# Query, key and value projections as seven products of quarters, with the first norm's residual affine on GpSimd and the adjacency check on ScalarE

## The chip, the cores and the metric

The kernel runs on one core of one Trainium2 chip. The metric is the device time of one launch in microseconds (us). A core has a matrix engine (TensorE, PE in the profile, with its weight loads listed apart as PEld), a vector engine (VectorE, DVE), an activation engine (ScalarE, ACT), a general engine (GpSimd, POOL) and a queue engine that issues most transfers (SyncE, SP). Each engine works through its own instructions in order and waits on semaphores for the others. All data are 32-bit floats, apart from the adjacency, which is int32.

## What is computed

64 graphs of 256 nodes with 256 features go through a graph-attention layer (two attentions, two norms, a feed-forward block) and then through a relational attention layer, again with two norms and a feed-forward block. What the change touches is the start of the second layer and the norm of the first:

```python
# layer 0, after its two graph attentions
h = _layernorm(residual + h, g_ln1, b_ln1)
residual2 = h
ff = jnp.matmul(jax.nn.relu(jnp.matmul(h, w_ff1) + b_ff1), w_ff2) + b_ff2
src = _layernorm(residual2 + ff, g_ln2, b_ln2)
# layer 1
q = (src @ Wq + bq).reshape(Bb, Nn, h, dh).transpose(0, 2, 1, 3)
k = (src @ Wk + bk).reshape(Bb, Nn, h, dh).transpose(0, 2, 1, 3)
scores = jnp.einsum('bhid,bhjd->bhij', q, k) / np.sqrt(dh)
attn = jax.nn.softmax(scores, axis=-1)
for r in range(Wv.shape[0]):
    v_r = (src @ Wv[r] + bv[r]).reshape(Bb, Nn, h, dh).transpose(0, 2, 1, 3)
    mask = (adj_matrix == r)[:, None]
    out = out + jnp.einsum('bhij,bhjd->bhid', attn * mask, v_r)
```

There are 8 heads of 32 features. The adjacency holds only 0 and 1, so of the four relations two matter.

## The kernel before

`narrow_path` does the work. It assumes that the adjacency holds 0 and 1 and that no exponential overflows; it sums up evidence against that, and `general_path` runs as well if there is any.

**Tiling.** Two graphs (512 nodes) are one unit; there are 32 units. A tile has 128 partitions. Features-first tiles (`hT`) have two blocks of 128 features, each with 512 nodes; nodes-first tiles (`y`, `v`) have four blocks of 128 nodes.

**The loop.** `turn(y_, x_, z)` is called 32 times. It takes unit y_ through layer 1, unit x_ = y_+1 through the feed-forward block of layer 0, and unit z = y_+2 through the graph attentions, and weaves the three together. Within a turn the order on PE, SP, DVE and ACT is the program's own, written out by hand (`manual_schedule`); GpSimd is ordered by the framework. The last turn has no x_, and there only PE and SP have the written order.

**The start of a turn** is what the change rewrites. `query(0)`, `query(1)`, `key(0)`, `key(1)` (`projection`, L986) each multiply two 128x128 weight blocks with 512 nodes into one PSUM bank, and ACT copies the bank out while it adds the bias (L988). `scores(0)` (L1015) makes the scores of the first four heads of the first graph, and ACT takes their exponentials (L1021). `values` (L999) multiplies four blocks of nodes with 512 weight columns, and DVE adds the bias row on the way out (L1001). The norm of unit x_ is applied by ACT (`applied_norm`, L828), DVE transposes it (L668), and twelve transfers and four GpSimd copies put the blocks in place (L685). The residual's affine, y*g+b, is on DVE: `times` (L837) here and `plus` (L840) later in the turn. `masks(n)` (L1026) multiplies exponentials with the adjacency, `totals(n)` (L1031) adds the two halves of nodes, and `sums(n)` (L1041, L1044) multiplies both with the values and with ones. `first(...)` are steps of the feed-forward block's hidden layer.

**Seven products.** `hidden_seven` (L871, L880, L883) and `HiddenOut` (L960, L968) already multiply two by two quarters with seven instead of eight products. Their sums of weight quarters are formed once (`seven`, `seven_out`), those of the data in every turn by DVE (L854, L946).

**PSUM.** Of eight banks six rotate under the tag "g"; "po" and "zo" are one bank each and take the attention's sums.

**The check** (`checked`, L706) is one DVE instruction per unit near the end of a turn: the sum of (a-1)*a over the adjacency, which is 0 for zeros and ones.

**Weights.** The second norm's scale and shift of layer 0 are folded into the weights of layer 1 at the start (`folding`): `scaled` on GpSimd, `shifted` by small products.

Of the kernel before, what the change touches and what calls it, by code (L numbers as in the profile page):

```python
# [16 lines left out]
P = 128  # L17
# [368 lines left out]
def narrow_path(  # L386
# [123 lines left out]
    def gat_weights():  # L510
# [5 lines left out]
        a1, a2 = columns([v.rearrange("f o -> (f o)") for v in (g_a1, g_a2)], "ga", nc.scalar, "k")  # L516
# [31 lines left out]
    lg1, lb1, bf1, lg2, lb2, bq, bk, lg3, lb3, b1 = columns(  # L548
        (g_g1, g_b1, g_bf1, g_g2, g_b2, t_bq, t_bk, t_g1, t_be1, t_b1), "cols", nc.scalar, "q")
    rg1, rb1, rg2, rb2 = row(g_g1, "rg1"), row(g_b1, "rb1"), row(g_g2, "rg2"), row(g_b2, "rb2")  # L550

    wq, wk, wo = weight(t_Wq, "wq"), weight(t_Wk, "wk"), weight(t_Wo, "wo")
# [4 lines left out]
    rbv = row(t_bv[0:2].rearrange("r f -> (r f)"), "rbv")  # L557
    nc.vector.tensor_tensor(wv[:, :, 1, :], wv[:, :, 1, :], wv[:, :, 0, :], ALU.subtract)
    nc.vector.tensor_tensor(rbv[:, F:], rbv[:, F:], rbv[:, :F], ALU.subtract)
# [3 lines left out]
    def seven(w, name):  # L563


        h = FF // 2
# [34 lines left out]
    wf1s, wf2s, w1s, w2s = [], [], [], []  # L601

    def folding():
# [8 lines left out]
        for w, bias, name in ((wq, bq, "bq"), (wk, bk, "bk")):  # L612
            shifted(w, range(KB), lb2, bias, name)
            scaled(w, lg2)
        yield
        ps = bank("rbvp")
        for k in range(KB):
            nc.tensor.matmul(ps, lb2[:, k:k + 1].to_broadcast([P, P]), wv[:, k].rearrange("p r f -> p (r f)"),
                             start=(k == 0), stop=(k == KB - 1))
        nc.vector.tensor_tensor(rbv, rbv, ps, ALU.add)  # L620
        scaled(wv.rearrange("p c r f -> p c (r f)"), lg2)
# [12 lines left out]
    for n, (rb, v) in enumerate(((rb1, g_bf2), (rb2, t_bo), (rb3, t_b2))):  # L634
        nc.gpsimd.tensor_add(rb, rb, row(v, None, rows[:, n, :F]))

# [25 lines left out]

    def normed_features(u, l, xn, natural=False, queues=(nc.sync,)):
# [7 lines left out]
        if natural:  # L671
            hT = work.tile([P, KB, TN], F32, tag="hT", name=f"hT{u}_{l}")
            to = hT.rearrange("c k (t a r) -> c (k t) a r", a=Q, r=32)
            for q in range(Q):
                for a in range(Q):
                    move = nc.gpsimd.tensor_copy if q == a else nc.sync.dma_start
                    move(to[q * 32:(q + 1) * 32, :, a], yt[a * 32:(a + 1) * 32, q].rearrange("c k t r -> c (k t) r"))  # L677
            return [hT[:, k] for k in range(KB)]
# [25 lines left out]
    def checked(u, aq):  # L704
        a = aq.rearrange("p t n -> p (t n)")
        nc.vector.scalar_tensor_tensor(a, a, 1.0, a, op0=ALU.subtract, op1=ALU.mult,  # L706
                                       accum_out=other[:, u:u + 1])
# [20 lines left out]
    class Softmax:  # L728

        def __init__(s, u, l, wh, rows, c):  # L730
            s.u, s.wh, s.rows, s.c = u, wh, rows, c
            s.s = (work.tile([P, T, N], F32, tag="s", name=f"s{u}_{l}", bufs=1) if u > 1 else
# [98 lines left out]
    def affine(y, g_, b_):  # L831

        times(y, g_)
        plus(y, b_)

    def times(y, g_):
        nc.vector.tensor_mul(y, y, g_[:, None, :].to_broadcast(list(y.shape)))  # L837

    def plus(y, b_):
        nc.vector.tensor_add(y, y, b_[:, None, :].to_broadcast(list(y.shape)))  # L840
# [138 lines left out]
    def projection(u, hT, name, w, c):  # L979

        d = work.tile([P, KB, TN], F32, tag=name, name=f"{name}{u}", bufs=1)

        def step(m):
            ps = bank(f"{name}p{u}_{m}")
            for k in range(KB):
                nc.tensor.matmul(ps, w[:, k, m * P:(m + 1) * P], hT[k],  # L986
                                 start=(k == 0), stop=(k == KB - 1))
            nc.scalar.activation(d[:, m, :], ps, AF.Identity, bias=c[:, m:m + 1])  # L988

        return d, step  # L990

    def values(u, hT, blocks, v=None):
        if v is None:
            v = work.tile([P, T, 2 * F], F32, tag="v", name=f"v{u}", bufs=1)
        wvf = wv.rearrange("p c r f -> p c (r f)")
        for t in blocks:
            ps = bank(f"vp{u}_{t}")
            for k in range(KB):
                nc.tensor.matmul(ps, hT[k][:, t * P:(t + 1) * P], wvf[:, k, :],  # L999
                                 start=(k == 0), stop=(k == KB - 1))  # L1000
            nc.vector.tensor_tensor(v[:, t, :], ps, rbv, ALU.add)  # L1001
        return v
# [3 lines left out]
    def weighted(u, b, m, q, k_, aT):  # L1006
# [13 lines left out]
        for a in range(HPB):  # L1020
            mark[f"exp{b * KB + m}"] = nc.scalar.activation(e[:, a, :], ps[a], AF.Exp, scale=isd)  # L1021
        return b, m, ab, e, ea
# [24 lines left out]
    def divided(u, b, po, zo, oT):  # L1047


        rz = work.tile([P, KB * N], F32, tag="s" if u < NG - 1 else "yt", name=f"rz{u}_{b}", bufs=1)  # L1050
# [62 lines left out]
    def out_pieces(u, y, h1):  # L1113

        if u == NG - 2:
            s = [work.tile([P, T, N], F32, tag="s", name=f"sq{u}", bufs=1),
# [38 lines left out]
    def turn(y_, x_, z):  # L1155
# [3 lines left out]
        q, query = projection(y_, hT, "q", wq, bq)  # L1159
        k_, key = projection(y_, hT, "k", wk, bk)  # L1160
        oT = q
        acc = [None] * G
        e = {}

        def scores(n):
            e[n] = weighted(y_, *quads[n], q, k_, Y["aT"])
# [31 lines left out]
        with order:  # L1198
            query(0)
            query(1)  # L1200
            if X:
                applied_norm(X["y"], *X.pop("n"))
            last = norm(waiting[0][0], 3, waiting[0][1]) if waiting else None
            key(0)
            key(1)
            if X:
                X["hT"] = normed_features(x_, 0, X["y"])
                times(X["y"], rg1)
            scores(0)
            if z + 1 < NG:  # L1210
                load_x(z + 1)
            if X:
                masks(0)
                totals(0)
# [278 lines left out]
```

## Time and profile before

| | |
|---|---|
| Time of the launch | 3075.3 us, median of 3 runs (3073.74 to 3075.54) |
| Profiled execution | span 3072.8 us |
| One turn, from one first query product to the next (1510.36 to 1604.16) | 93.80 us |
| PEld busy | 2330.1 us (76%) |
| DVE busy | 2595.7 us (84%) |
| ACT busy | 1602.2 us (52%) |
| POOL busy | 648.0 us (21%) |
| Granted TensorE clock, mean | 0.995 |
| L837 y*g on DVE, 128x1024 | 126 times, mean 1263 ns |
| L840 y+b on DVE, 128x1024 | 126 times, mean 1302 ns |
| L706 check on DVE, 128x1024 | 30 times, mean 1216 ns |
| L685 GpSimd copy, 32x256 | 386 to 1442 ns, median 400 |

An engine's busy time is the union of its instructions' durations. Matrix instructions overlap in the pipe, so what one costs is read from the distance of starts and not from its duration. A 32-bit product appears as two records: 512 records of L999 are 32 turns times four blocks of nodes times two blocks of features times two.

### The profile page before, as it was taken

How to read it: one execution, taken by the hardware profiler on the slowest of the kernel's cores; microseconds unless marked ns; L12 is line 12 of the kernel's file. 1: busy time of each engine (PE TensorE's matmuls, PEld its weight loads, DVE VectorE, ACT ScalarE, POOL GpSimd, SP SyncE). 2: the span in 40 equal slices, each digit the busy share in tenths (PEclk: the TensorE clock that was granted, in tenths of full speed). 3: DMA queues.
4: the chain of work that ended last, by engine and by line, in shares of the span. 5: the costliest groups of instructions: out<-in, count | busy, mean ns of one | idle time of the engine just before them, and what ended most of it. 6: DMA issues, size and time to landing. Idle time of an engine off the chain costs nothing.

```text
span 3072.8 us, 56424 instructions
## 1 busy us (share of the span) xinstructions
PE 3031.3 (99%) x21432; PEld 2330.1 (76%) x21432; DVE 2595.7 (84%) x4890; ACT 1602.2 (52%) x3212; POOL 648.0 (21%) x896
## 2 busy tenths in 40 slices
PE   7999999999999999999999999999999999999998
PEld 6677877778777778777787777787777787777866
DVE  4788888888888888888888888888888888888876
ACT  4455545555545555555555455555455554554553
POOL 3122121222211221212221112222112212122211
PEclk8999999999999999999999999999999999999999
DMA  5011111211111211112211112111112111121000
GB/s 149 13 37 35 34 39 25 44 41 35 35 35 32 44 37 32 39 26 43 44 33 35 40 25 44 37 36 35 30 38 44 35 34 39 25 44 37 18 13 16
DMA packets 427988, 113.37 MB, mean 37 GB/s; under 512 B 364568, under 2 KB 427072, under 8 KB 427712
## 3 DMA queue, kind: packets, MB, share of 16 engines
q1 hardware_dynamic: 417664, 102.46, 15.8%
q10 hardware_dynamic: 8992, 6.19, 0.8%
q8 instruction: 172, 2.82, 0.4%
q0 software_dynamic: 1056, 1.05, 0.1%
q14 instruction: 104, 0.85, 0.1%
HBM read 57.04 MB, written 16.78 MB: 24 GB/s over the span
## 4 chain that ended last, share of the span: by engine, by line
PE 90%; DVE 7%; DMA 1%; POOL 1%; ACT 1%; issue 0%; SPq 0%; ACTq 0%; POOLq 0%; DVEq 0%
PE yf L960 22%; PE h1a L871 15%; PE h1b L871 11%; PE po L1041 8%; PE vp L999 7%; PE sp L1015 4%; PE xpp L715 4%; PE yop L786 4%; PE qp L986 3%; PE kp L986 3%; PE ygp L786 3%; PE zo L1044 2%; PE hpp L775 2%; DVE s L750 2%; DVE yt L668 1%; DVE eaq L946 1%
## 5 line engine op out<-in xcount | busy, mean ns | idle before, releaser
L880 ACT COPY h<-h1b 128x512 f32<-128x512 f32 x384 | 224.6, 585 | 390.0 <-PE h1b L871 390.0
L828 ACT ACTIVATE y<-y,nm,rs 128x256 f32<-128x256 f32 x450 | 239.0, 591 | 238.4 <-DVE nm L821 234.1
L883 DVE TENSOR_TENSOR h<-h1a,h 128x512 f32<-128x512 f32 x384 | 263.6, 687 | 117.5 <-PE h1a L871 111.6
L1026 DVE TENSOR_TENSOR ea<-e,aT 128x1024 f32<-128x1024 f32 x256 | 309.5, 1239 | 54.3 <-ACT e L1021 54.3
L1021 ACT ACTIVATE e<-sp 128x512 f32<-128x512 f32 x512 | 264.3, 602 | 52.0 <-PE sp L1015 48.7
L1054 POOL TENSOR_TENSOR low<-low,rq 128x16 f32<-128x16 f32 x64 | 13.9, 218 | 1087.3 <-DVE rq L1053 1087.3
L685 POOL COPY hT<-yt 32x256 f32<-32x256 f32 x244 | 207.2, 849 | 59.0 <-DVE yt L668 51.4
L968 DVE TENSOR_TENSOR y<-yf,y 128x256 f32<-128x256 f32 x448 | 183.1, 409 | 39.7 <-PE yf L960 39.6
L999 PE MATMUL vp<-wv,hT 128*128 128x512 f32 x480 | 214.0, 599 | 0.0
L801 DVE BATCH_NORM_STATS2 st<-y 128x6 f32<-128x256 f32 x512 | 207.7, 408 | 5.5
L812 POOL TENSOR_SCALAR rs<-mv 128x4 f32<-128x4 f32 (+1 forms) x134 | 34.2, 255 | 720.7 <-DVE mv L802 454.6
L999 PEld LDWEIGHTS vp<-wv,hT 128*128 128x128 f32 x480 | 88.7, 190 | 110.4 <-issue 103.2
L840 DVE TENSOR_TENSOR y<-y,rb 128x1024 f32<-128x1024 f32 (+1 forms) x130 | 166.9, 1284 | 3.2
L988 ACT ACTIVATE q<-qp,cols 128x512 f32<-128x512 f32 x64 | 44.0, 687 | 238.3 <-PE qp L986 238.3
L914 ACT ACTIVATE h<-h,cols 128x512 f32<-128x512 f32 x256 | 167.0, 714 | 1.5 <-DVE h L883 1.1
L837 DVE TENSOR_TENSOR y<-y,rg 128x1024 f32<-128x1024 f32 (+1 forms) x130 | 161.8, 1245 | 2.2 <-ACT y L828 1.1
L1031 DVE TENSOR_TENSOR es<-e 128x1024 f32<-128x1024 f32 x128 | 155.5, 1215 | 0.0
L677 POOL COPY hT<-yt 32x256 f32<-32x256 f32 x120 | 115.6, 964 | 169.2 <-DVE yt L668 159.7
L1015 PEld LDWEIGHTS sp<-q,k 32*128 32x128 f32 x2048 | 92.5, 184 | 74.2 <-issue 44.8
L1015 PE MATMUL sp<-q,k 32*128 32x256 f32 x2048 | 146.6, 400 | 2.0 <-ACT k L988 2.0
L1041 PE MATMUL po<-e,v 128*32 128x256 f32 x2048 | 136.3, 384 | 0.0
L813 POOL TENSOR_TENSOR rs<-rs,mhalf 128x4 f32<-128x4 f32 (+1 forms) x134 | 134.5, 1004 | 8.2
(249 smaller groups left out, 7191.4 us busy)
## 6 DMA issues: line engine op xcount, KB each, us to landing
hT<-yt SPq DMA_DIRECT2D x912, 32.0 KB, 2.0
y<-in_x_dram SPq DMA_DIRECT2D x32, 512.0 KB, 4.7
xq<-in_x_dram SPq DMA_DIRECT2D x240, 64.0 KB, 2.2
aq<-in_adj_dram SPq DMA_DIRECT2D x240, 64.0 KB, 2.4
out_dram<-y SPq DMA_DIRECT2D x30, 512.0 KB, 2.9
hT<-yt ACTq DMA_DIRECT2D x180, 32.0 KB, 1.9
wf<-in_L_gnn_w_ff_dram SPq DMA_DIRECT2D x2, 1024.0 KB, 8.1
w<-in_L_gnn_W_dram SPq DMA_DIRECT2D x2, 1024.0 KB
```

Of the source, the lines that this page charges most:

```text
L786: nc.tensor.matmul(ps[:, i * F:(i + 1) * F], lhs(t, k), rhs(b, k), start=(k == 0), stop=(k == n - 1))
L801: nc.vector.bn_stats(st[:, t, :], y[:, t, :])
L828: mark["normed"] = nc.scalar.activation(y[:, t, :], y[:, t, :], AF.Identity, bias=nm[:, t:t + 1], scale=rs[:, t:t + 1])
L871: nc.tensor.matmul(ps[:, i * N:(i + 1) * N], w_[:, f * P:(f + 1) * P], m, start=first and i == 0, stop=True, skip_group_check=True)
L880: mark["copied"] = nc.scalar.copy(out(h, o, b), pair(ps))
L883: mark["added"] = nc.vector.tensor_tensor(out(h, o, b), pair(one[h]), out(h, o, b), ALU.add)
L960: nc.tensor.matmul(s.ps[n][:, i * F2:(i + 1) * F2], a[:, k, i * P:(i + 1) * P], w_[:, k, :], start=n in (1, 2, 5) and i == 0 and k == 0, s ...
L999: nc.tensor.matmul(ps, hT[k][:, t * P:(t + 1) * P], wvf[:, k, :], start=(k == 0), stop=(k == KB - 1))
L1015: nc.tensor.matmul(ps[a][:, j * N:(j + 1) * N], k_[hp, m, j0:j0 + P], q[hp, m, b * N:(b + 1) * N], start=True, stop=True)
L1021: mark[f"exp{b * KB + m}"] = nc.scalar.activation(e[:, a, :], ps[a], AF.Exp, scale=isd)
L1026: nc.vector.tensor_tensor(ea[:, a:a + 2, :], e[:, a:a + 2, :], ab[:, None, :].to_broadcast([P, 2, NB * N]), ALU.mult)
L1041: nc.tensor.matmul(po[hp, m * N:(m + 1) * N], vs[:, hp], w[:, a, j * N:(j + 1) * N], start=(n == 0), stop=(n == len(terms) - 1))
```

## The change

Query, key and value are made by a class `Projections`. The weights of query and key are joined to one 256x512 matrix, those of the two relations' values to another, and each is multiplied with the unit's features as two by two quarters, in seven products. One product is two 128x128 blocks times 256 columns. Results go through two PSUM banks: for query and key two of "g", for the values "zo" and "po". ACT copies four times per matrix, DVE adds three times. Four sums of data quarters are made by DVE at the start of a turn. The biases are no longer added on the way out: one feature row of the data (partition 96 of the second block) is set to 1 by GpSimd (`with_ones`), and the weights' row there holds the bias. Since normalized features sum to zero, that feature's weights are subtracted from all rows first (`joined`). The steps of the start are woven anew. Both parts of the residual's affine after the first norm go to GpSimd. The check is an ACT instruction, Square of a-0.5 with an accumulator, which is 0.25 for each zero or one; it stands earlier, behind the second softmax's exponentials. Two buffers are shared anew (tags "s" and "k" go).

```diff
+    def joined(w, name, bias):
+        ps, pr = bank(f"{name}bp"), bank(f"{name}rp")
+        for k in range(KB):
+            nc.tensor.matmul(ps, lb2[:, k:k + 1].to_broadcast([P, P]), w[:, k],
+                             start=(k == 0), stop=(k == KB - 1))
...
+        nc.tensor.matmul(pr, only.to_broadcast([P, P]), w[:, KB - 1], start=True, stop=True)
+        nc.vector.tensor_tensor(bias, bias, ps[one].rearrange("p (o f) -> p o f", o=2), ALU.add)
+        for k in range(KB):
+            nc.vector.scalar_tensor_tensor(w[:, k], w[:, k], lg2[:, k:k + 1], pr,
+                                           op0=ALU.mult, op1=ALU.subtract)
...
-        for w, bias, name in ((wq, bq, "bq"), (wk, bk, "bk")):
-            shifted(w, range(KB), lb2, bias, name)
-            scaled(w, lg2)
+        joined(wqk, "wqk", brow[:, 0:2])
+        wqks.extend(seven(wqk, "wqk"))
         yield
...
+        joined(wvf, "wv", brow[:, 2:4])
+        wvs.extend(seven(wvf, "wv"))
...
+    def with_ones(hT):
+        nc.gpsimd.memset(hT[KB - 1][one], 1.0)
+        return hT
...
     def checked(u, aq):
         a = aq.rearrange("p t n -> p (t n)")
-        nc.vector.scalar_tensor_tensor(a, a, 1.0, a, op0=ALU.subtract, op1=ALU.mult,
-                                       accum_out=other[:, u:u + 1])
+        nc.scalar.activation(a, a, AF.Square, bias=mhalf[:, 0:1], accum_out=other[:, u:u + 1])
...
-            s.s = (work.tile([P, T, N], F32, tag="s", name=f"s{u}_{l}", bufs=1) if u > 1 else
+            s.s = (work.tile([P, T, N], F32, tag="v", name=f"s{u}_{l}", bufs=1) if u > 1 else
...
+    def affine(y, g_, b_, engine=None):
+        engine = engine or nc.vector
+        engine.tensor_mul(y, y, g_[:, None, :].to_broadcast(list(y.shape)))
+        engine.tensor_add(y, y, b_[:, None, :].to_broadcast(list(y.shape)))
...
+        def sums(s):
+            tt = work.tile([P, HPB, NB * N], F32, tag="e", name=f"tq{s.u}").rearrange("p a n -> p (a n)")
+            s.t = [tt[:, n * N:(n + 1) * N] for n in range(4)]
+            for n, (x_, y_) in enumerate(((s.h[0][1], s.h[0][0]), (s.h[1][1], s.t[0]),
+                                          (s.h[1][1], s.h[0][1]), (s.h[1][0], s.t[1]))):
+                nc.vector.tensor_tensor(s.t[n], x_, y_, ALU.subtract)
...
+        def copied(s, x, o, b, ps):
+            nc.scalar.copy(s.out(x, o, b), ps.rearrange("p (i n) -> p i n", i=2))
+        def added(s, x, o, b):
+            y = s.out(x, o, b)
+            nc.vector.tensor_tensor(y, s.one[x].rearrange("p (i n) -> p i n", i=2), y, ALU.add)
+        def step(s, x, n):
+            a11, a12, a22, s1, s2, s3, s4 = wqks if x == "q" else wvs
+            w, m = {1: (a11, s.h[0][0]), 2: (a12, s.h[1][0]), 5: (s1, s.t[0]), 3: (s4, s.h[1][1]),
+                    6: (s2, s.t[1]), 7: (s3, s.t[2]), 4: (a22, s.t[3])}[n]
...
+            ps = (s.two if n in (2, 5, 3) else s.one)[x]
+            for i in range(2):
+                l, r = (w[:, i * P:(i + 1) * P], m) if x == "q" else (m[:, i * P:(i + 1) * P], w)
+                nc.tensor.matmul(ps[:, i * N:(i + 1) * N], l, r, start=n in (1, 2, 5) and i == 0, stop=True,
+                                 skip_group_check=True)
+            if n == 2:
+                s.copied(x, 0, 0, ps)
+                s.added(x, 0, 0)
+            elif n == 5:
+                s.copied(x, 1, 1, ps)
+            elif n == 3:
+                s.copied(x, 0, 1, ps)
+            elif n == 6:
+                s.added(x, 0, 1)
+            elif n == 7:
+                s.added(x, 1, 1)
+            elif n == 4:
+                s.copied(x, 1, 0, ps)
...
         with order:
-            query(0)
-            query(1)
+            p.sums()
+            p("q1 v1 q2")
             if X:
-                applied_norm(X["y"], *X.pop("n"))
+                applied_norm(X["y"], *X["n"], [0, 1])
             last = norm(waiting[0][0], 3, waiting[0][1]) if waiting else None
-            key(0)
-            key(1)
+            p("v2 q5")
             if X:
+                applied_norm(X["y"], *X.pop("n"), [2, 3])
                 X["hT"] = normed_features(x_, 0, X["y"])
-                times(X["y"], rg1)
-            scores(0)
+                affine(X["y"], rg1, rb1, nc.gpsimd)
+            scores(0, ())
+            p("v5")
+            powers(0, (0, 1))
             if z + 1 < NG:
                 load_x(z + 1)
-            if X:
-                masks(0)
-                totals(0)
-            v = values(y_, hT, range(0, T // 2))
...
+            p("q3 v3")
+            masks(0, (0,))
+            powers(0, (2, 3))
             if waiting:
                 applied_norm(waiting[0][1], *last)
-            if X:
-                v = values(y_, hT, range(T // 2, T), v)
+            p("q6 v6 q7 v7")
+            masks(0, (2,))
+            totals(0)
+            p("q4 v4")
             steps = first_hidden(x_) if X else None
             scores(1)
...
+            masks(1)
+            totals(1)
             if Z:
                 early(z)
-            masks(1)
-            totals(1)
             sums(0)
...
-            if X:
-                plus(X["y"], rb1)
             scores(3)
...
             Z["m"].exp(0)
             Z["m"].exp(1)
+            checked(z, Z["aq"])
+            if z + 1 < NG:
+                load_adjacency(z + 1)
             out.add(5)
...
             affine(X["y"], rg2, rb2)
             out(7)
-            checked(z, Z["aq"])
-            if z + 1 < NG:
-                load_adjacency(z + 1)
```

## The prediction

> **What bounds the kernel now.** I read the page's busy times first, then the chain that ended last, then the turn that begins at 1510.36 us in the chain and in the engines' timelines.
>
> ```profile
> PE 3031.3 (99%) x21432; PEld 2330.1 (76%) x21432; DVE 2595.7 (84%) x4890; ACT 1602.2 (52%) x3212; POOL 648.0 (21%) x896
> ...
> PE 90%; DVE 7%; DMA 1%; POOL 1%; ACT 1%; issue 0%; SPq 0%; ACTq 0%; POOLq 0%; DVEq 0%
> ```
>
> The matrix engine is the bound; DVE is next, with 79 us of work in a turn of 93.8. A busy PE says little about its efficiency, so the price of a product is read from the chain, whose pieces are distances between starts (start, us, what, records):
>
> ```profile
> 1510.36 3.44 PE qp L986 x8
> 1513.80 3.43 PE kp L986 x8
> 1517.23 1.08 PE sp L1015 x16
> 1518.31 7.07 PE vp L999 x16
> 1525.37 1.07 PE sp L1015 x16
> 1526.45 1.86 PE po L1041 x32
> ...
> 1536.05 0.86 PE h1a L871 x4
> ```
>
> A record of 512 columns takes 0.43 us (3.44/8), one of 256 takes 0.215 (0.86/4). The values take 7.07 and not 16 x 0.43 = 6.88: the first product behind the scores' narrow ones pays about 0.17. The start of the turn up to the attention's first sums is 16.09 us with no gap.
>
> Where DVE has room there is shown by its waits (start, us, and in brackets the idle time before):
>
> ```profile
> 1606.84 0.16 DVE L821 SCALAR_TENSOR_TENSOR nm<-mv,rs 128x4 f32<-128x4 f32 x1 [1.24 <-POOL rs L813]
> ...
> 1613.24 2.58 DVE L1026 TENSOR_TENSOR ea<-e,aT 128x1024 f32<-128x1024 f32 x2 [1.20 <-ACT e L1021]
> ...
> 1628.85 0.72 DVE L1052 STREAM_TRANSPOSE rz<-zo 128x512 f32<-128x512 f32 x1 [2.36 <-PE zo L1044]
> ```
>
> Up to the second sums of a turn DVE is 2.4 us ahead of PE, and after that it works without a pause. So a saving on PE must keep within what DVE and ACT can follow in those first 24.6 us.
>
> **What the skill says.** "TensorE: Matmul & The Clock Gate", Back-to-back issue gap, has a warm product cost its columns at 2.4 GHz plus 2.5 ns. Halving the width therefore loses next to nothing, and the 0.43 and 0.215 above agree. "SBUF — State Buffer", Who interferes with whom, says that a DVE instruction with two SBUF inputs and a GpSimd instruction that reads SBUF exclude each other, for the whole instruction. The trace agrees, at its start:
>
> ```profile
> 43.69 1.74 POOL L570 TENSOR_TENSOR wf1s<-wf1s,wf 128x512 f32<-128x512 f32 x1
> 45.39 1.71 POOL L572 TENSOR_TENSOR wf<-wf 128x512 f32<-128x512 f32 x1
> ...
> 45.90 1.49 DVE L750 SCALAR_TENSOR_TENSOR s<-s,aT 128x256 f32<-128x256 f32 x1
> 47.32 0.08 DVE L750 DVE_READ_ACCUMULATOR s<-s,aT 128x1 f32 x1
> 47.32 1.48 DVE L750 SCALAR_TENSOR_TENSOR s<-s,aT 128x256 f32<-128x256 f32 x1
> 48.73 0.08 DVE L750 DVE_READ_ACCUMULATOR s<-s,aT 128x1 f32 x1
> 48.73 0.41 DVE L750 SCALAR_TENSOR_TENSOR s<-s,aT 128x256 f32<-128x256 f32 x1
> ```
>
> The same DVE instruction takes 0.41 us alone and 1.49 beside a two-input GpSimd one of 512 elements: that one holds the port about 1.0 us, and it gets it between two DVE instructions. "ScalarE: Activation LUTs", Table sets, says that cheap functions lie in every set; it does not name Square there.
>
> **The projections on PE.** Removed: 3.44 + 3.43 + 7.07 = 13.94 us. Added: 2 x 7 products of 4 records, 56 x 0.215 = 12.07, and 0.17 behind the scores. Gross gain 1.70 us a turn, 54 us in 32 turns, if nothing waits.
>
> **What PE waits for instead.** I lay out the new start by the written order, counted from its first product (0.86 us a product, 0.2 from a release to the product that needed it, as a freed PSUM bank also has its weights to load).
> Products q1, v1, q2, v2, q5 end at 4.31; the scores end at 5.39. ACT copies q2 from 2.63 to 3.22 (0.59, as L880), DVE adds until 3.95 (0.69, as L883), then makes nm (0.16), and only then may ACT apply two blocks of the norm (0.59 + 0.49) ahead of v2's copy, which ends at 5.75. v5 writes the bank that this copy frees: it starts at 5.93 where 5.56 was possible. Loss 0.37.
> v3 needs v5's copy, which stands behind the norm's other two blocks and ends at 7.80: loss 0.35.
> q7 needs DVE's add for q6; ahead of it in DVE's order stand the first mask (1.2), which waits for two exponentials (to 8.85), and nm. The add ends at 10.9, q7 starts at 11.05 instead of 10.6: loss 0.45, or 0.77 if GpSimd copies take the port ahead of the mask and of nm. I take 0.45.
> The rest of the row has its adds in time. The second scores end at 15.6, the first sums start there instead of at 16.09: of the 1.70 some 0.5 is left (0.2 with the high value).
>
> **DVE and ACT beside it.** DVE gains work in this stretch: four sums (1.7, from four times L854's 0.42) and six adds of 0.69 for four of 0.68 (+1.4), less `times` (1.26). That uses up the lead of 2.4 but not more. `plus` (1.30) and the check (1.22 + 0.08) also leave DVE, in places where PE does not wait for it, so I count no gain. With the check gone from the turn's end DVE reaches the four sums about 1 us earlier, in time for q5. ACT gets eight copies for four (8 x 0.59 - 4 x 0.68 = 2.0 us) and the check, about 1 us by the spacing of its 512-element rows. The check falls into this hole:
>
> ```profile
> 1597.56 1.71 ACT L766 ACTIVATE hp<-hp,z 128x256 f32<-128x256 f32 x4 [3.86 <-DVE z L754]
> ```
>
> If Square needed another table, 1.28 us more fits there, and the load back for the next exponentials falls before the next turn's first copy. SP gets the adjacency's eight transfers earlier; behind them on SP there is nothing until the next norm's twelve, a turn's start later. The ones row on GpSimd comes some 12 us before its use. So both: nothing.
>
> **The affine on GpSimd.** No row shows a two-input GpSimd instruction of 1024 elements beside DVE work. From 1.27 us at 512 elements with 1.0 of it on the port I estimate 2.3 us with 2.0 on the port, each. They follow the four copies: transposes end near 8.25, copies near 10.8 (0.4 each, one shut out by the mask), multiply until 13.2, add until 15.5. The multiply meets DVE at adds that read PSUM, which have one SBUF input and pass. The add meets the second half of the masks, due at 13.5, and holds it until about 15.3. Then masks end at 16.5 and totals at 17.7; PE wants them at 16.5 and 17.4. So 0.15 to 0.35 is lost; none with 1.6 on the port, 0.85 with 2.3. I take 0.2. The hidden layer's four sums and the next masks then run without a gap and end about when the second sums need them.
>
> **Start and sum.** `joined` adds six wide products (12 records, 5.2 us) and drops 16 one-column records (0.115 each) and four wide ones (3.7 together); GpSimd forms eight sums of 0.85 where it scaled for 3.8. I count +1 us once. Per turn 0.5 - 0.2 = 0.3, for 31 turns 9.3; the last turn has no affine and may keep 1.0. Sum: 9.3 + 1.0 - 1 = 9.3 us off the profiled span of 3072.8. The launch's median lies 2.5 above that span, which I keep: 3075.3 - 9.3 = 3066.
>
> **The rivals.**
> Slower: the affine's add holds the port for 2.3 us or starts later, the q7 wait is at its high end, and each hand-over costs a little more. The mechanism is one: DVE gets to `masks` and `totals` too late for the first sums. It decides once DVE is delayed more than the 1.7 us of lead that it has there. With 0.2 left of the gain and 0.6 lost, +0.4 x 31 = 12 us: 3088. For it speaks the port in the trace; against it, that PE's own waits before the sums give DVE time.
> No difference: waits give back all of the 1.70, 3075. For it speaks that every hand-over above is within 0.3 us of being in time or late.
> Large gain: the waits at v5 and v3 do not arise as laid out (ACT a little earlier) and the port is free; 1.3 of 1.70 stays, 40 us: 3035. Against it, ACT's written order.
> The change does not do what it says: if the new check counted wrongly, the general path would run as well, far above all of this.
>
> **Chances.** A measurement of this kernel tells about 0.2%, 6 us, from no change. Forecast (a gain of 6 to 25 us) 0.40; large gain 0.10; no difference 0.17; slower by DVE's delay 0.32; general path 0.01. Faster 0.50, same 0.17, slower 0.33. The range 3040 to 3093 leaves out the upper end of the large gain and delays above 0.6 us a turn; the forecast's own range is 3050 to 3069.
>
> **What would show it.** PE's first row: 56 records in about 13.4 us with gaps before v5, v3 and q7. DVE: a mask or total of 1.2 us drawn out to 2.5 to 3.5 beside a GpSimd add. The first sums 15.4 to 16.0 us after the turn's start, the second ending at 24.2 to 24.6 (24.62 now). A turn of 93.5 us. I am wrong if PE waits in the feed-forward steps have changed too, if tables are loaded more than 64 times, or if GpSimd's instructions take over 3 us.

## The result: slower by 0.3%, where a gain was forecast

| | before | after |
|---|---|---|
| Time of the launch, median of 7 runs each on one chip | 3074.53 us (3073.05 to 3076.28) | 3083.82 us (3082.2 to 3085.53) |
| Profiled span | 3072.8 us | 3083.0 us |
| A turn, median of turns 1 to 29 | 93.44 us | 93.63 us |
| First sums start, from the turn's first product | 16.18 us | 15.80 us |
| `zo` of the first pair ends | 18.54 us | 18.74 us |

The ratio is 1.003, with a 95% interval of 1.002 to 1.004. The forecast was 3066; the slower case had 3088. Positions in a turn are here read from the engines' timelines, where the old first sums start at 16.18 us and not at 16.09, as the chain has it.

The profiled spans differ by 10.2 us. Start of the first turn: 0.44 us earlier. First turn: 1.25 longer. The 29 turns behind it: 0.19 each by their medians, 5.5, and 0.9 more in single longer turns. Last turn but one: 0.2 longer. Last turn: 2.7 longer. The parts come to 10.1, and rounding explains the rest.

DVE's group of totals on the page of the kernel before:

```profile
L1031 DVE TENSOR_TENSOR es<-e 128x1024 f32<-128x1024 f32 x128 | 155.5, 1215 | 0.0
```

On the page of the kernel after, the busy times, the share of each engine in the chain, and the same group:

```profile
PE 3011.8 (98%) x22192; PEld 2459.0 (80%) x22192; DVE 2626.4 (85%) x4963; ACT 1684.3 (55%) x3404; POOL 845.3 (27%) x992
...
PE 80%; DVE 13%; SPq 2%; issue 2%; ACT 2%; DMA 1%; POOL 1%; DVEq 0%; POOLq 0%; ACTq 0%
...
L1095 DVE TENSOR_TENSOR es<-e 128x1024 f32<-128x1024 f32 x128 | 220.9, 1726 | 0.0
```

PE's busy time fell by 19.5 us although the launch became longer, and DVE's share of the chain rose from 7% to 13%. The totals are about half of that rise (3% of the chain on that page). One took 1215 ns on average before and takes 1726 now; 128 of them make 65 us, which is 2.1 us for one total in each of 31 turns. In the trace it is the first total of a turn: in turns 1 to 29 it takes 3.38 to 3.40 us, and the second takes 1.22.

The chain of waits of the kernel after, for a turn (start, us, what):

```profile
1609.25 0.87 PE qk L1046 x4
1610.12 0.86 PE v L1046 x4
...
1623.14 0.58 SPq L713
1623.72 0.04 issue
1623.76 0.06 SPq L713
1623.83 3.32 DVE es L1095
1627.15 0.04 issue
1627.19 0.64 PE zo L1108 x8
```

A product of four records costs the expected 0.86 to 0.88 us where nothing waits. What ends last is no product but the first pair's total: 3.32 us on DVE, for which PE's `zo` waits. SP's transfers stand ahead of it in the chain but don't release it: the total reads exponentials alone.

The timeline of the same turn shows what draws the total out (start, us, engine, line, what; in brackets the idle time before). The first product starts at 1609.09:

```profile
1614.91 1.13 PE L1046 MATMUL v<-wvs,tq 128*128 128x256 f32 x4 [0.18 <-ACT v L1029]
...
1617.43 2.75 POOL L711 COPY hT<-yt 32x256 f32<-32x256 f32 x4 [0.49 <-DVE yt L694]
...
1619.97 1.13 PE L1046 MATMUL qk<-tq,wqk 128*128 128x256 f32 x4 [0.26 <-DVE qk L1033]
1620.26 2.36 POOL L859 TENSOR_TENSOR y<-y,rg 128x1024 f32<-128x1024 f32 x1
1622.61 1.21 DVE L1090 TENSOR_TENSOR ea<-e,aT 128x1024 f32<-128x1024 f32 x1
1622.69 3.36 POOL L860 TENSOR_TENSOR y<-y,rb 128x1024 f32<-128x1024 f32 x1
1623.74 3.39 DVE L1095 TENSOR_TENSOR es<-e 128x1024 f32<-128x1024 f32 x1
1627.19 0.64 PE L1108 MATMUL zo<-es,ones 128*32 128x256 f32 x8 [0.37 <-DVE es L1095]
```

GpSimd's multiply (L859) takes 2.36 us, and the add (L860) is issued 0.08 us behind the second half of the mask. The mask passes in its usual 1.21 us; the add waits for it and takes 3.36. The total, queued behind the mask, then waits for the add: 3.39 us for an instruction of 1.22. So the port (the access to SBUF that the two engines share, as the prediction has it) goes back and forth, and each side waits once for nearly the whole of the other's instruction.

### The profile page after: what moved, and what is told of

Same layout as the page of the kernel before. It is cut to its first block, busy times and chain, and to the rows that moved or that the text cites. A ratio compares the mean times of both kernels' runs of the same rounds, so it can differ in the third digit from the quotient of the medians.

```text
span 3083.0 us, 58504 instructions
## 1 busy us (share of the span) xinstructions
PE 3011.8 (98%) x22192; PEld 2459.0 (80%) x22192; DVE 2626.4 (85%) x4963; ACT 1684.3 (55%) x3404; POOL 845.3 (27%) x992
## 4 chain that ended last, share of the span: by engine, by line
PE 80%; DVE 13%; SPq 2%; issue 2%; ACT 2%; DMA 1%; POOL 1%; DVEq 0%; POOLq 0%; ACTq 0%
PE yf L980 22%; PE h1a L891 15%; PE h1b L891 11%; PE po L1105 6%; PE qk L1046 4%; PE xpp L740 4%; PE yop L811 4%; PE ygp L811 3%; PE v L1046 3%; DVE es L1095 3%; PE sp L1077 2%; PE zo L1108 2%; PE hpp L800 2%; SPq L713 2%; DVE yt L694 2%
## 5 line engine op out<-in xcount | busy, mean ns | idle before, releaser
L1029 ACT COPY qk<-qk 128x512 f32<-128x512 f32 x128 | 75.4, 589 | 287.6 <-PE qk L1046 287.6
L1095 DVE TENSOR_TENSOR es<-e 128x1024 f32<-128x1024 f32 x128 | 220.9, 1726 | 0.0
L1077 PE MATMUL sp<-qk 32*128 32x256 f32 x2048 | 146.6, 400 | 0.1
L742 ACT COPY xp<-xpp 128x260 f32<-128x260 f32 x128 | 45.5, 386 | 171.6 <-PE xpp L740 171.5
L1033 DVE TENSOR_TENSOR qk<-qk,qk 128x512 f32<-128x512 f32 x96 | 65.9, 687 | 84.1 <-ACT qk L1029 64.9
L891 PE MATMUL h1a<-tt,wf 128*128 128x256 f32 x512 | 134.2, 386 | 0.0
L1105 PE MATMUL po<-ea,v 128*32 128x256 f32 x2048 | 134.2, 379 | 0.0
L980 PEld LDWEIGHTS yf<-wf,eaq 128*128 128x128 f32 x1024 | 119.1, 192 | 16.1 <-DVE eaq L966 14.9
```

The lines of the kernel that those rows point to most:

```text
L891: nc.tensor.matmul(ps[:, i * N:(i + 1) * N], w_[:, f * P:(f + 1) * P], m, start=first and i == 0, stop=True, skip_group_check=True)
L980: nc.tensor.matmul(s.ps[n][:, i * F2:(i + 1) * F2], a[:, k, i * P:(i + 1) * P], w_[:, k, :], start=n in (1, 2, 5) and i == 0 and k == 0, s ...
L1077: nc.tensor.matmul(ps[a][:, j * N:(j + 1) * N], k_[hp, m, j0:j0 + P], q[hp, m, b * N:(b + 1) * N], start=True, stop=True)
L1095: mark[f"summed{b * KB + m}"] = nc.vector.tensor_add(es, e[:, :, 0:N], e[:, :, N:2 * N])
L1105: nc.tensor.matmul(po[hp, m * N:(m + 1) * N], vs[:, hp], w[:, a, j * N:(j + 1) * N], start=(n == 0), stop=(n == len(terms) - 1))
```

## The experiments

Every kernel has 4 to 21 runs; the kernel before ran beside it on the same chip (19 to 28 runs), and the ratio is to those. "Turn" is the median of turns 1 to 29 of the profiled execution, "excess" what those turns have above 29 times that median (2.4 in the kernel after, 1.5 in the kernel before), "sums" and "zo" the start of the first sums and the end of the first pair's `zo`. In the expectations P is the theory that GpSimd holds the port when DVE needs it, F that the features land too late for the hidden layer, W that the written order makes PE wait.

| Run | Median, us | Ratio (95%) | Turn | Excess | Sums | zo |
|---|---|---|---|---|---|---|
| no_affine | 3070.91 | 0.9988 (0.9981 to 0.9995) | 93.07 | 9.6 | 15.79 | 18.16 |
| affine_late | 3082.82 | 1.0026 (1.0016 to 1.0037) | 93.63 | 2.3 | 15.80 | 18.74 |
| affine_dve | 3090.89 | 1.0053 (1.0039 to 1.0066) | 93.91 | 2.2 | 16.65 | 19.01 |
| before_affine_pool | 3172.72 | 1.0321 (1.0307 to 1.0335) | 96.11 | 17.5 | 18.84 | 21.21 |
| affine_low | 3072.51 | 0.9992 (0.9984 to 1.0) | 93.06 | 7.2 | 15.79 | 18.16 |
| add_low | 3070.27 | 0.9985 (0.9979 to 0.9992) | 93.05 | 6.5 | 15.79 | 18.16 |
| affine_low_feat | 3088.31 | 1.0045 (1.0031 to 1.0059) | 93.80 | 0.6 | 15.79 | 18.16 |
| affine_low_q7 | 3081.05 | 1.0018 (1.001 to 1.0027) | 93.53 | 1.3 | 15.53 | 17.89 |
| affine_low_last | 3087.32 | 1.004 (1.0027 to 1.0054) | 93.80 | 0.1 | 15.80 | 18.16 |
| affine_low_third | 3067.29 | 0.9973 (0.9962 to 0.9984) | 93.06 | 1.3 | 15.80 | 18.16 |
| affine_low_best | 3044.87 | 0.9901 (0.9886 to 0.9916) | 92.40 | 1.7 | 15.14 | 17.50 |
| before_check_act | 3073.49 | 0.9993 (0.9985 to 1.0001) | 93.44 | 1.1 | 16.18 | 18.54 |

### The affine left out

no_affine leaves the affine after the first norm out of the turns (it computes with g = 1 and b = 0 there).

```diff
                 X["hT"] = normed_features(x_, 0, X["y"])
-                affine(X["y"], rg1, rb1, nc.gpsimd)
```

> The changed kernel without the residual's affine after the first norm in the turns (y*g+b is left out there; g is 1 and b is 0 in these inputs). Theory P (port): what is lost on PE in front of the first sums' zo products is DVE's totals(0) held by GpSimd's add (3.3 us for 1.2). Then totals(0) is 1.2 us again, zo does not wait, the second sums end about 24.4 us after the turn's start (24.97 now), the turn falls by 0.5 and the time to about 3066. Theory F (features late): the twelve transfers of unit x_, issued one behind the other at 0.6 us each from 8 us on, land at 18.5, and the hidden layer's first product and sums wait for them anyway. Then totals(0) is 1.2 us too, but a wait of 0.3 to 0.5 us moves to the product behind the sums, the second sums end at 24.8 or later and the time stays at 3079 to 3084.

The typical turn is 0.56 us shorter than after, all of it at the first pair's `zo` (18.16 against 18.74); the first sums themselves start where they did. That is the port's price. But 13 of 29 turns were longer than typical by more than 0.15 us, and the excess of 9.6 us, where after has 2.4, took nearly half of the gain back. One of those turns in the timeline:

```profile
1610.91 7.54 SPq L713 DMA_DIRECT2D hT<-yt  x12
...
1620.10 0.61 PE L1108 MATMUL zo<-es,ones 128*32 128x256 f32 x8
...
1621.98 0.43 DVE L874 TENSOR_TENSOR tt<-hT 128x256 f32<-128x256 f32 x1 [3.55 <-issue]
...
1622.00 1.10 PE L891 MATMUL h1b<-hT,wf 128*128 128x256 f32 x4 [1.28 <-issue]
1622.44 0.43 DVE L874 TENSOR_TENSOR tt<-hT,tt 128x256 f32<-128x256 f32 x1
```

PE is through with `zo` and stands still for 1.28 us; PE's hidden layer and DVE's differences begin together, at 1622.0. What both read is `hT`, and both wait on semaphores of the twelve transfers that SP issued until 1618.5. The trace doesn't record when the last of them landed, so that they land late is read from this start; whether the long turns come from it is asked below.

### Where the affine stands

affine_dve puts both parts back on DVE, at their places in the kernel before.

```diff
-                affine(X["y"], rg1, rb1, nc.gpsimd)
+                nc.vector.tensor_mul(X["y"], X["y"], rg1[:, None, :].to_broadcast([P, T, F]))
...
             first("4a 7b rb")
+            if X:
+                nc.vector.tensor_add(X["y"], X["y"], rb1[:, None, :].to_broadcast([P, T, F]))
```

> The changed kernel with the affine back on DVE at its two old places. P: the multiply (1.2 us) stands ahead of the first mask, which has only 0.5 us of idle time before it; so the mask, the add for q7 and q7 come 0.7 us later, the first sums start at 16.4 and totals(0) takes 1.2; the second sums end about 24.9 to 25.1, time 3082 to 3088, no better than the changed kernel. F: the same, with the transfers landed in time; 3082 to 3088. If it is faster than 3075, the move to GpSimd is the whole loss and my layout of the mask is wrong.

7 us more than after: the multiply, 1.22 us on DVE ahead of the first mask, moved the first sums from 15.80 to 16.65. So in this order of work GpSimd was the better engine for the affine even at the bad place.

before_affine_pool does that one move in the kernel before.

```diff
-                times(X["y"], rg1)
+                nc.gpsimd.tensor_mul(X["y"], X["y"], rg1[:, None, :].to_broadcast([P, T, F]))
+                nc.gpsimd.tensor_add(X["y"], X["y"], rb1[:, None, :].to_broadcast([P, T, F]))
...
-            if X:
-                plus(X["y"], rb1)
```

> The kernel before with only the affine moved to GpSimd. P: masks(0) and totals(0) are drawn out by up to 2 us each beside the two GpSimd instructions, but DVE leads PE by 2.4 us there and loses times (1.26), so PE waits at most 0.3 us a turn: 3072 to 3084. F: no change, 3072 to 3077.

The expectation missed by some 90 us. In its timeline both masks of the first pair wait for the port, one behind each GpSimd instruction:

```profile
1661.48 2.35 POOL L1208 TENSOR_TENSOR y<-y,rg 128x1024 f32<-128x1024 f32 x1
...
1662.05 6.15 DVE L1026 TENSOR_TENSOR ea<-e,aT 128x1024 f32<-128x1024 f32 x2 [2.46 <-ACT e L1021]
...
1663.91 3.21 POOL L1209 TENSOR_TENSOR y<-y,rb 128x1024 f32<-128x1024 f32 x1
...
1669.99 1.72 PE L1015 MATMUL sp<-q,k 32*128 32x256 f32 x12 [1.38 <-DVE v L1001]
```

Two masks take 6.15 us where the kernel before shows 2.58. Behind them in DVE's queue stand the values' adds, which free PSUM banks, and PE's second scores wait 1.38 us for the first of these. The first sums start 2.66 us later. DVE's idle time in front of the masks lies before they can start, and so covers nothing.

affine_late moved the affine's text behind the second division, with the framework told to queue it behind a DVE instruction.

```diff
-                affine(X["y"], rg1, rb1, nc.gpsimd)
...
             if Z:
                 shares(1)
+            if X:
+                with behind("divided1"):
+                    affine(X["y"], rg1, rb1, nc.gpsimd)
```

> The affine stays on GpSimd but behind the second shares, where DVE for some 8 us runs nothing with two SBUF inputs. P and F both: the two GpSimd instructions take about 2.4 us each and no DVE instruction beside them is drawn out; time within 2 us of the run without the affine: P 3066, F 3079 to 3084. If this one is slower than that run by over 4 us, the affine costs by something else than the port.

Nothing moved: the multiply still stands in front of the first pair's second mask and the total takes 3.39 us. GpSimd is ordered by the framework, and naming a DVE instruction did not hold the affine back. The run tells nothing of the theories. affine_low names a GpSimd instruction instead:

```diff
-        nc.gpsimd.tensor_add(low, low, rq)
+        mark["low"] = nc.gpsimd.tensor_add(low, low, rq)
...
-                affine(X["y"], rg1, rb1, nc.gpsimd)
...
             if Z:
                 shares(1)
+            if X:
+                with behind("low"):
+                    affine(X["y"], rg1, rb1, nc.gpsimd)
```

> The change, with its affine on GpSimd queued behind GpSimd's small sum `low` (L1118) of the second graph, where VectorE has some 6 us of work that reads PSUM or one tile only. Theory P (what was lost is the port, held while VectorE had the first mask and totals(0) to do): first sums 15.8 us after the turn's first product, totals(0) back at 1.2 us, zo of the first pair ends at 18.16, a typical turn 93.05, 3069 to 3073 us, as with the affine left out (3070.9). Theory S (the affine's 4.4 us of port have to be paid somewhere, wherever it stands): the turn keeps 93.6 or more, 3080 to 3086.

P holds for the typical turn, and S falls there. At the new place GpSimd and DVE don't delay each other (timeline of affine_low):

```profile
1645.02 2.36 POOL L859 TENSOR_TENSOR y<-y,rg 128x1024 f32<-128x1024 f32 x1
1645.48 0.69 DVE L1121 TENSOR_TENSOR qk<-po,rz 128x512 f32<-128x512 f32 x1
1646.09 0.68 DVE L814 TENSOR_TENSOR y<-yop,y 128x512 f32<-128x512 f32 x1
...
1647.45 2.37 POOL L860 TENSOR_TENSOR y<-y,rb 128x1024 f32<-128x1024 f32 x1
1647.89 1.21 DVE L681 STREAM_TRANSPOSE aT<-aq 128x1024 int32<-128x1024 int32 x1
1649.07 0.69 DVE L814 TENSOR_TENSOR y<-yop,y 128x512 f32<-128x512 f32 x1
```

Add and multiply both take 2.36 us, and DVE's instructions, which read PSUM or a single tile, their usual time. This is what the Trainium skill has in "SBUF — State Buffer", Who interferes with whom: with at most one SBUF input, and outside its two-port modes, DVE doesn't contend with GpSimd.

The place is free only while the other work in the turn stays the same. In the last turn but one, where no unit is left for the graph attentions, one of the quarter sums (L966, two SBUF inputs) stands beside the affine's add:

```profile
2950.57 2.35 POOL L860 TENSOR_TENSOR y<-y,rb 128x1024 f32<-128x1024 f32 x1
...
2951.01 2.99 DVE L966 TENSOR_TENSOR eq<-h 128x1024 f32<-128x1024 f32 x1
```

That sum takes 1.19 us in no_affine, and the turn takes 76.86 us for 73.44 there; how much of these 3.4 us the held sum makes wasn't separated. affine_low_best has the same sum at 3.00 us, and so still pays there.

add_low moves only the add there and leaves the multiply at its place (the same `behind`, around the one instruction).

> The change, with only the affine's add queued behind GpSimd's small sum `low` (L1118) of the second graph, as in affine_low, and its multiply left where the change has it, in front of the first pair's second mask. Theory A (the multiply runs beside adds that read PSUM and costs nothing, the loss is the add's alone): totals(0) at 1.22 us, zo of the first pair ends at 18.16, 3070 to 3075 us. If the multiply delays that mask or the adds before it: zo ends at 18.4 to 19, 3077 to 3083.

zo at 18.16: at that place the multiply costs nothing, and the loss is the add's alone.

```profile
1612.62 2.36 POOL L1276 TENSOR_TENSOR y<-y,rg 128x1024 f32<-128x1024 f32 x1
1613.50 0.69 DVE L1033 TENSOR_TENSOR qk<-qk,qk 128x512 f32<-128x512 f32 x1 [0.62 <-PE qk L1046]
...
1614.97 1.21 DVE L1090 TENSOR_TENSOR ea<-e,aT 128x1024 f32<-128x1024 f32 x1
1616.11 1.22 DVE L1095 TENSOR_TENSOR es<-e 128x1024 f32<-128x1024 f32 x1
```

The multiply ends at 1614.98, when the mask begins.

### What is late next

affine_low_feat gives the features room, by moving the third scores and the second sums ahead of the first three hidden products.

```diff
-            steps = first_hidden(x_) if X else None
             scores(1)
             masks(1)
             totals(1)
+            steps = first_hidden(x_) if X else None
...
-            first("2a 1a 5a", 1)
             scores(2)
             sums(1)
+            first("2a 1a 5a", 1)
```

> affine_low with the third scores and second sums ahead of the hidden layer's first three products on TensorE, and that layer's four differences behind the second mask and total on VectorE. Theory F (with the port free, turns are lengthened by features that land late: 12 of 28 by 0.2 to 1.7 us with the affine left out, together 9 us): all turns within 0.2 us of 93.0, 3060 to 3064 us. If the lengthening has another cause (a wait of VectorE or of the cores' memory that does not go through those features), 3068 to 3073 and the same spread of turns.

Both halves came, one unforeseen: the excess fell from 7.2 to 0.6 us, so F is right about the long turns, but every turn is 0.74 us longer. The timeline has the price:

```profile
1632.36 1.11 PE L891 MATMUL h1b<-tt,wf1s 128*128 128x256 f32 x4
...
1634.14 1.13 PE L891 MATMUL h1b<-hT,wf1s 128*128 128x256 f32 x4 [0.68 <-ACT h L900]
```

The fifth and the third product use one PSUM bank, with ACT's copy between them. The second sums had filled that time. affine_low_third therefore moves the third scores alone:

```diff
-            first("2a 1a 5a", 1)
-            scores(2)
+            scores(2, ())
+            first("2a 1a 5a", 1)
+            powers(2, range(HPB))
             sums(1)
```

> affine_low with the third scores alone (not their exponentials, not the second sums) ahead of the hidden layer's first three products on TensorE, and that layer's four differences behind the second mask and total. The products get 1.1 us more for the features to land, and the second sums still stand between the fifth and the third product. Theory F (late features alone lengthen the turns of affine_low): typical turn 93.05 as there, turns above 93.4 at most 3 instead of 9, 3062 to 3067 us. If the new place costs a wait as in affine_low_feat (0.7 us in front of the third product): 93.7, 3083 to 3089.

As theory F had it: 93.06, excess 1.3, three long turns, and about 5 us less than affine_low. In affine_low_feat and here, giving the features more time removed most of the excess; why they are late in some turns stays open.

### The written order

affine_low_q7 is affine_low_feat with the first mask behind the adds.

```diff
             p("q3 v3")
-            masks(0, (0,))
             powers(0, (2, 3))
...
             p("q6 v6 q7 v7")
-            masks(0, (2,))
+            masks(0, (0, 2))
             totals(0)
```

> affine_low_feat with the first mask behind the adds of q7 and v7 instead of ahead of the adds of q6 and v6. Theory W (the written order costs: q7 waits 0.45 us for an add that stands behind that mask): first sums at 15.35 us instead of 15.80, turns 0.4 us shorter than affine_low_feat, 12 us in all. If the mask and total are then what ends last, the first sums start at 15.4 but zo of the first pair still ends at 18.1: no difference to affine_low_feat beyond 3 us.

0.27 us a turn of the 0.45, and 7 us in all; the first sums start at 15.53. The wait at q7 was real, and part of it is left: from v6 to q7 it is now 1.02 us instead of 1.29, and 0.86 would be without a wait. From v5 to v4 most products still take about 0.97 us.

affine_low_last queues the sums over quarters (L966) behind the adds in the last turn, where DVE isn't ordered by hand.

```diff
-        end.sums(1, 2, 4, 3)
+        with behind("fourth") if u == NG - 2 else ExitStack():
+            end.sums(1, 2, 4, 3)
...
-            nc.vector.tensor_tensor(y, s.one[x].rearrange("p (i n) -> p i n", i=2), y, ALU.add)
+            mark["fourth"] = nc.vector.tensor_tensor(y, s.one[x].rearrange("p (i n) -> p i n", i=2), y, ALU.add)
```

> affine_low_feat with the four sums over the hidden layer's quarters (L966), which VectorE takes up between the adds of the last turn, queued behind the adds of q6 and v6 of that turn. If these sums are why the last turn's first sums started at 19.4 us instead of 16.5: 2.5 to 3.5 us less than affine_low_feat, first sums of the last turn at 16 to 17. If they only take the place of the masks: within 1 us of affine_low_feat.

The last turn's first sums start at 16.89 instead of 18.27 us. Of these 1.38 us 0.57 are lost again by the second pair's `zo`, and 0.81 stay on PE to the end of the turn. The medians differ by 1.0 us with overlapping runs, so neither 2.5 us nor nothing: the quarter sums explain a part of the last turn's loss. In these profiled runs that turn takes 86.77 us for 87.44, and 86.10 in the kernel before.

affine_low_best joins affine_low_third, the mask of affine_low_q7, the quarter sums of affine_low_last, and this:

```diff
             if X:
-                applied_norm(X["y"], *X["n"], [0, 1])
-            last = norm(waiting[0][0], 3, waiting[0][1]) if waiting else None
-            p("v2 q5")
+                blocks, mv, rs, nm = X["n"]
+                nc.vector.scalar_tensor_tensor(nm, mv[:, :, 0], -1.0, rs, op0=ALU.mult, op1=ALU.mult)
+            p("v2")
+            if X:
+                applied_norm(X["y"], *X["n"], [1, 0])
+            p("q5")
             if X:
                 applied_norm(X["y"], *X.pop("n"), [2, 3])
                 X["hT"] = normed_features(x_, 0, X["y"])
+            last = norm(waiting[0][0], 3, waiting[0][1]) if waiting else None
...
+            p("q6 v6")
             if waiting:
                 applied_norm(waiting[0][1], *last)
-            p("q6 v6 q7 v7")
+            p("q7 v7")
```

`nm` is formed ahead of v2, and the block order [1, 0] keeps `applied_norm` from forming it again.

> affine_low_third with, beside it, the first mask behind the adds of q7 and v7, v2's copy ahead of the norm on ScalarE, the transposes of the features ahead of the waiting graph's moments, and the last turn's quarter sums behind the adds of q6 and v6. Theory W (the written order costs 0.45 us at q7 and 0.18 at v5): first sums at 15.3 us, turns of 92.5, 3045 to 3052 us. If the tail of two interleaved products (0.97 us a product, each waiting for the add before it) sets the first sums anyway: 15.5 and 92.8, 3052 to 3060.

3044.87 us in 4 runs, 1.0% below before (interval 0.8 to 1.1%), and the only one of these kernels with a gain of that size. In its timeline the turn begins at 1586.38:

```profile
1591.95 1.13 PE L1046 MATMUL v<-wvs,tq 128*128 128x256 f32 x4
...
1596.60 1.13 PE L1046 MATMUL qk<-tq,wqk 128*128 128x256 f32 x4
...
1599.24 2.35 DVE L1090 TENSOR_TENSOR ea<-e,aT 128x1024 f32<-128x1024 f32 x2
...
1601.51 1.22 DVE L1095 TENSOR_TENSOR es<-e 128x1024 f32<-128x1024 f32 x1
...
1601.52 1.07 PE L1105 MATMUL po<-e,v 128*32 128x256 f32 x16
```

v5 starts 5.57 us into the turn (5.82 after), q7 at 10.22 (10.88), and neither has an idle time in front of it; mask and total, behind all adds, are still in time for the sums that read them. Of the 1.70 us of products saved, 1.04 now reach the end of the turn. v2's earlier copy and the later moments were not run on their own, so what each gives isn't told apart.

### The check alone

before_check_act is the kernel before with the check on ScalarE.

```diff
-        nc.vector.scalar_tensor_tensor(a, a, 1.0, a, op0=ALU.subtract, op1=ALU.mult,
-                                       accum_out=other[:, u:u + 1])
+        nc.scalar.activation(a, a, AF.Square, bias=mhalf[:, 0:1], accum_out=other[:, u:u + 1])
```

> The kernel before with the check of the adjacency on ScalarE alone, at the place that the change gives it. Theory as predicted (1.3 us of idle VectorE and 1.8 us of idle ScalarE, no table loads): 3073 to 3077 us, turns of 93.4. If the activation there delays the exponentials or copies of the next turn, or brings two table loads a turn: 3095 us or more.

No change that can be told (0.9985 to 1.0001), with the same turn to the hundredth. In the kernel after the tables are loaded 64 times, as before (groups of ScalarE):

```profile
L934 ACT ACT_TABLE_LOAD x32 | 41.1, 1283 | 0.6
L771 ACT ACT_TABLE_LOAD x30 | 38.5, 1283 | 0.5
L727 ACT ACT_TABLE_LOAD x1 | 1.3, 1283 | 8.0 <-DMA colsr<-in_L_gnn_b_ln_dram 8.0
L1086 ACT ACT_TABLE_LOAD x1 | 1.3, 1283 | 0.0
```

## Where the prediction failed

**The step that failed** is the term for the affine's add on the port: "So 0.15 to 0.35 is lost; none with 1.6 on the port, 0.85 with 2.3. I take 0.2." It cost 0.58 us a turn (zo at 18.74 with it, 18.16 with the add or the whole affine elsewhere). With 0.58 in place of 0.2 the forecast's -0.3 a turn becomes +0.08; in 31 turns that is 11.8 of the 19.5 us between the forecast span and the measured one. The mechanism was named and the hold was nearly right: 2.0 us was estimated, and the total shows 3.39 - 1.22 = 2.17. So was the lead of 1.7 us that DVE had there: 2.17 - 0.58 leaves 1.6. The prediction's own times, a total at 17.7 that was wanted at 17.4, already gave 0.3; it took 0.2. What the step had wrong beside this was who comes first. It let the add begin at 13.2, ahead of the mask, so that only the mask would wait. The copies ended 0.3 us later (11.1 for 10.8), the add was issued at 13.60 and the mask at 13.52, so the mask went first, the add waited 1.0 us for it, and the total behind the mask paid the whole hold. The total ends at 18.04 instead of the forecast 17.7. The Trainium skill's rule in "SBUF — State Buffer", Who interferes with whom, that the pair is held for the whole instruction, fits: 2.17 of the add's 2.36 us. The prediction's own sign of being wrong, a GpSimd instruction of over 3 us, came true with the add's 3.36.

**The first sums.** Laid out: v5 at 5.93, q7 at 11.05, sums at 15.6, 0.5 us earlier than before. Measured: 5.82, 10.88, 15.80, 0.38 earlier. v5 lost 0.26 us (laid out: 0.37) and q7 0.43 (0.45). No wait of v3's own shows (laid out: 0.35), but q3, v3 and q6 start 0.11 us late each. Not in the layout were products 0.95 to 0.97 us apart from q7 to the second scores, where two products alternate and each waits for the add before it; that took about 0.4 us, and the shorter waits ahead of it gave 0.15 back. The prediction also says that its 0.43 and 0.215 us agree with the price in the Trainium skill, "TensorE: Matmul & The Clock Gate", Back-to-back issue gap. Estimated by that page's formula, 512 and 256 columns take 0.216 and 0.109 us, half of what the trace has for a record; what agrees is that half the width costs half. The sum used the measured prices, so the forecast doesn't rest on this.

**The turns.** -0.3 forecast, +0.19 measured: 0.12 from the first sums, 0.38 from the port, less 0.01 of rounding. The slower case is what came true, in place and mechanism, and its price of 0.6 for the delay was nearly the measured one. That its 3088 lies near 3083.82 is partly luck: it had +0.4 a turn, 12 us, where the typical turns gave 5.5, and the rest came from the first and last turns, which it did not have.

**The last turn** was to keep 1.0 us; it lost 2.7. It has no affine, but there DVE isn't ordered by hand and takes four quarter sums of 1.2 us and two masks ahead of q6's add, so that PE stood still for 1.86 us in front of q7. The forecast carried the per-turn gain over to a turn with another order.

**The start** was to cost 1 us. The first turn began 0.44 us earlier, at 103.87; in the other kernels with this start it began at 102.6 to 104.1, so neither sign can be told.

**Not asked at all** was when the twelve transfers land. With the port in the way it hardly mattered (2.4 us of excess after); without it, late features cost 6 to 10 us, as much as the forecast's whole gain. A forecast without the port term would have failed here: it would have promised some 15 us, and no_affine is 4 us below before.

**Right:** the check, the multiply beside adds that read PSUM, the prices of ACT's copies (0.59 us) and DVE's adds (0.69). Open: why the first turn is 1.25 us longer and the next 1.1, and why what waits for the twelve transfers starts up to 1.9 us later in a long turn.

## What to carry to other kernels

When an element-wise pair goes to GpSimd, look for a stretch where VectorE reads PSUM or one tile, pin it there by an instruction of GpSimd itself, and look at the turns that differ from the rest; here the loss was decided by which DVE instruction stood behind the pair and not by GpSimd's load (27% busy). When products of quarters replaced wide ones here, most of the saving was lost in the hand-overs: between two products that share a bank there must be enough other work for the copy or add, and what DVE does for later stages belongs behind those adds. After each stall removed, ask what is the next to arrive late, and test the same change with that moved too.

## What the runs showed of the hardware

- A GpSimd add or multiply with two SBUF inputs of 128x1024 took 2.36 us undisturbed (affine_low), and the add delayed a DVE add with two SBUF inputs, queued behind it, by 2.17 (after). It took the port between two DVE instructions that were queued without a gap, and a DVE instruction took it between two of GpSimd: in before_affine_pool the two masks took 6.15 us for 2.58, one waiting for the multiply and one for the add.
- Square over 128x1024 int32 with an accumulator took ACT 1.13 to 1.14 us and 0.19 for the read of the accumulator (after), and brought no table load: there are 64 with it and without it.
